# Rotary rotation inside PSUM, signs in the bank of sums, and three moves in the order of a post-norm transformer block

## The chip, the cores and the metric

The kernel runs on one core of a Trainium2 chip. The core has five engines with a queue of instructions each: TensorE (PE: matrix products, with its weight loads shown as PEld), VectorE (DVE), ScalarE (ACT), GpSimd (POOL) and SyncE (SP), which here only issues transfers. GpSimd issues transfers too, on a second queue. Matrix products are written to PSUM, eight banks of 128 partitions x 512 numbers of 32 bits; all other data on the core are in SBUF. The metric is the device time of one execution in microseconds (us), as the median over runs.

## The reference

One block: attention with 16 heads of width 32 that share one key and one value head, rotary positions on queries and keys, then a feed-forward part with ternary weights; a normalization without scale follows each. There are four batches (B = 4) of 512 positions (T = 512) and 512 channels (D = 512); the hidden width is 1408.

```python
q = (x @ Wq + bq).reshape(B, T, H, HD).transpose(0, 2, 1, 3)
k = (x @ Wk + bk)[:, None]
v = (x @ Wv + bv)[:, None]
q = _rotary(q, HD)
k = _rotary(k, HD)
scores = einsum('bhqd,bhkd->bhqk', q, broadcast(k)) / sqrt(HD)
attn = softmax(scores, axis=-1)
ctx = einsum('bhqk,bhkd->bhqd', attn, broadcast(v))
x = _layernorm(x + (ctx @ Wo + bo))
...
def _quantize(w):
    gamma = jnp.mean(jnp.abs(w))
    return jnp.clip(jnp.round(w / (gamma + EPS)), -1.0, 1.0)
hidden = sigmoid(x @ _quantize(w1).T) * (x @ _quantize(w2).T)
x = _layernorm(x + hidden @ _quantize(w3).T)
```

`_rotary` turns each pair (x1, x2) of the two halves of a head into (x1 cos - x2 sin, x2 cos + x1 sin).

## The kernel before, in words

**Main loop.** Work is cut into 64 steps (`steps`, line 678), numbered n: batch b, group of four heads c (NC = 4), chunk of 128 keys t (NT = 4). `PER` = 16 steps make a batch. In a step TensorE computes the scores of four heads with 128 keys (`scores`, line 375, tile `ps`), ScalarE takes the exponential (`es`), and TensorE weighs the values of the step before (`weigh`, tile `acc`). For the first batch TensorE also adds up the exponentials in every step (`count`, tile `den`); for the others GpSimd keeps running totals (`total`), and TensorE adds over them once in four steps (`normalize`, line 432).

**Maxima.** The softmax needs each row's maximum ahead of its scores. `find_maxima` (line 705) works LEAD = 7 steps ahead: TensorE computes the products (`pmax`), VectorE reduces them (`mx`). Called with two chunks, the products go to a tile of the pool `ps_sc`, whose two buffers of two banks serve the scores too; called with one, they go to the one bank tagged `den`, which also holds the sums. Line 763 chooses: two pairs per step while n < PER + 4, then single, pair, single.

**Projections.** `project_in` (line 237) makes keys, values and queries of a batch; its tiles `pk`, `pq` are in `ps_mm`, two buffers of one bank, which serve all other products too. `turn` (line 225) is the rotation. It gets the projection `src` in PSUM and a copy `r` (for the keys `kv`) that ScalarE makes in SBUF with the bias added. VectorE makes `a` = (src + bias) cos; after a yield it makes `w` = the copy with the halves of each head swapped (a shuffle), multiplies `w` by the signed sine, and adds `a` and `w`. The keys are stored four times, so a second addition writes the last 32 partitions.

**Fill.** `project_in`, `project_out` (line 517) and `feed_forward` (line 551) are generators; `Fill.draw` takes pieces of them between the fixed parts of a step, with about as much TensorE work as the step's `pace`. Each engine runs its instructions in the order of the program. `late` holds generators that `due` advances by one yield per slot, two slots a step: `spread` of the maxima, `normalize`, `layernorm`, `store_q`, `load_x`.

**Sums.** `normalize` copies the sums (`sums`), sends them through memory into a compact layout (`flat`, `few`), takes the reciprocal on VectorE, sends it back spread over the partitions (`rden`), and GpSimd multiplies `ctxT` by it. There is one yield between any two of these.

**Weights.** `quantized` (line 157) turns the three weight matrices, 11 tiles each, to ternary in 66 jobs: a first pass over each matrix sums absolute values on ScalarE (`junk`), a second takes the sign on ScalarE (`sgn`, bf16 in SBUF), and VectorE combines it (`raw`); the result is stored to memory (`kept`, the `w<-raw` transfers). GpSimd issues loads, four jobs ahead, and stores, from two pools of four and five buffers. Before the main loop, `quantize(3)` runs in each of seven rounds; inside, two or three jobs a step (lines 767, 769).

**Start.** SyncE issues the biases, `wkv_sb`, four `xT`, `wq_sb[0]`, `cos_sb`, `sin_sb`, and then the rest. GpSimd's first loads of `raw` stand right behind its memsets.

**End.** `feed_forward` splits the 11 hidden blocks into parts of 4, 4 and 3 (`parts`). For each block TensorE makes `gu` twice (gate and up), VectorE multiplies them (`hw`), and ScalarE and VectorE split the product into two halves `h`. After a part, TensorE multiplies it with the third matrix for the four tiles of 128 rows (`po`), and VectorE adds that to `x`. After the last part VectorE takes the statistics; in the last batch each tile is normalized and stored at once (`layernorm` with `root`).

Of the kernel before, what the change touches and what calls it, by code (L numbers as in the profile page):

```python
# [9 lines left out]
F32 = mybir.dt.float32  # L10
F32R = mybir.dt.float32r
BF16 = mybir.dt.bfloat16
# [7 lines left out]
P = 128  # L20
HD = 32
# [6 lines left out]
def postln_block(  # L28
# [75 lines left out]
    bq_sb = const.tile([P, NC], F32, name="bq_sb")  # L104
    bkv_sb = const.tile([P, 1], F32, name="bkv_sb")
    bo_sb = const.tile([P, D], F32, name="bo_sb")

    class Batch:
# [48 lines left out]
    def quantized():  # L157

        order = ((0, False), (1, False), (0, True), (2, False), (1, True), (2, True))
        jobs = [(m, last, f) for m, last in order for f in range(NF)]

        means = {}
        for n, (m, last) in enumerate(order):
            if not last:
                for k, step in ((2, 0), (6, 1), (10, 2)):
                    means[(n + 1) * NF + k] = (m, step)
        raws, part, row, pg, hi, waiting = {}, {}, {}, {}, {}, []

        def load(k):
            if k < len(jobs):
                m, _, f = jobs[k]

                tag, bufs = ("wd", 5) if k % 2 else ("wg", 4)
                raws[k] = wp.tile([P, W], F32, tag=tag, name="raw", bufs=bufs)
                pool.dma_start(out=raws[k], in_=wf[m, f])

        def mean(m, step):
            if step == 0:  # L180
                row[m] = small.tile([P, 1], F32, tag="row", name="row")
                dve.tensor_reduce(row[m], part[m], AX.X, ALU.add)
            elif step == 1:
                pg[m] = ps_mm.tile([P, 1], F32, tag="mm", name="pg")
                mm(pg[m], ones, row[m], True, True)
                gamma = small.tile([P, 1], F32, tag="gamma", name="gamma")
                act.activation(gamma, pg[m], AF.Identity, scale=1.0 / (NF * W * P), bias=eps_q)
                row[m] = gamma
            else:
                hi[m] = small.tile([P, 1], F32, tag="hi", name="hi")  # L190
                act.mul(hi[m], row[m], 0.5)

        AHEAD = 4
        for k in range(AHEAD):
            load(k)
        for k, (m, last, f) in enumerate(jobs):
            load(k + AHEAD)
            if k in means:
                mean(*means[k])
            raw = raws.pop(k)  # L200
            if not last:
                if f == 0:
                    part[m] = small.tile([P, NF], F32, tag="part", name="part", bufs=3)
                junk = work.tile([P, W], BF16, tag="th", name="junk")
                act.activation(junk, raw, AF.Abs, accum_out=part[m][:, f : f + 1])
            else:
                sgn = work.tile([P, W], BF16, tag="th", name="sgn")
                act.activation(sgn, raw, AF.Sign, bias=hi[m])
                dve.scalar_tensor_tensor(raw, raw, hi[m], sgn, ALU.is_gt, ALU.min)
                waiting.append((kept[m][f], raw))  # L210
            if len(waiting) > 2 or k + 1 == len(jobs):
                for w, q in waiting[: 1 if k + 1 < len(jobs) else 3]:
                    pool.dma_start(out=w.bitcast(F32), in_=q)
                del waiting[:1]
            yield
# [6 lines left out]
        act.copy(head, whole)  # L222
        pool.tensor_tensor(tail, whole, head.bitcast(F32), ALU.subtract)

    def turn(outs, src, bias, r, n):

        w = work.tile([P, T], F32, tag="rot_b", name="w")
        a = work.tile([P, T], F32, tag="rot_c", name="a", bufs=1)
        dve.scalar_tensor_tensor(a[0:n], src[0:n], bias[0:n], cos_sb[0:n], ALU.add, ALU.mult)
        yield  # L230
        dve.stream_shuffle(w[0:n], r[0:n], swap)
        dve.tensor_tensor(w[0:n], w[0:n], sin_sb[0:n], ALU.mult)
        for out, rows in outs:
            dve.tensor_tensor(out, a[rows], w[rows], ALU.add)
        yield

    def project_in(b):

        s = batches[b]
        n = P - HD  # L240
        while now < NC * NT * (b - 2):
            yield 0

        pk = ps_mm.tile([P, T], F32, tag="mm", name="pk")
        for c in range(NC):
            mm(pk, wkv_sb[:, c, :], s.xT[c], c == 0, c == NC - 1)
            if c == 1:
                yield -1.8
        kv = work.tile([P, T], F32, tag="rot_a", name="kv")
        act.activation(kv, pk, AF.Identity, bias=bkv_sb)  # L250
        s.kT = work.tile([P, T], F32, tag="kT", name="kT", bufs=3)
        rotation = turn(
            [(s.kT[0:n], slice(0, n)), (s.kT[n:P], slice(0, HD))], pk, bkv_sb, kv, n
        )
        next(rotation)
        yield 1.8
        next(rotation)
        if b > 0:
            late.append((slot + 2, split_k(b)))
        for c in range(NC):  # L260

            while b + 1 == B and c + 2 >= NC and not batches[0].projected:
                yield 0
            pq = ps_mm.tile([P, T], F32, tag="mm", name="pq")
            for d in range(NC):
                mm(pq, wq_sb[c][:, d, :], s.xT[d], d == 0, d == NC - 1)
                if d == 1:
                    yield -1.8
            r = work.tile([P, T], F32, tag="rot_a", name="r")
            act.activation(r, pq, AF.Identity, bias=bq_sb[:, c : c + 1])  # L270
# [7 lines left out]
            rotation = turn([(q, slice(0, P))], pq, bq_sb[:, c : c + 1], r, P)  # L278
            next(rotation)
            if c == 0:  # L280
                pv = ps_mm.tile([P, NT, HD], F32, tag="mm", name="pv")
                for t in range(NT):
                    transpose(pv[:, t, :], kv[n:P, ts(t, P)], ident[n:P, n:P])
                s.v = work.tile([P, NT, HD], F32, tag="v", name="v", bufs=3)
                act.copy(s.v, pv)
            yield 1.8
            next(rotation)
            if b > 0:
                late.append((slot + 2, store_q(b, c, q)))
            s.done = c + 1  # L290
        load_xT(NC if b == 0 else 2)

# [139 lines left out]
    def normalize(b, c):  # L432
# [12 lines left out]
        few = small.tile([P, NG * T // P], F32, tag="few", name="few")  # L445
        move(few, flat[0].rearrange("i (r j) -> (i r) j", r=HD))
        yield
        dve.reciprocal(few, few)
        move(flat[1].rearrange("i (r j) -> (i r) j", r=HD), few)
        yield  # L450
        rden = work.tile([P, T], F32, tag="rden", name="rden", bufs=1)
        for i in range(NG):
            move(rden[ts(i, HD), :], flat[1][i].partition_broadcast(HD))
        yield
        pool.tensor_tensor(s.ctxT[c], s.ctxT[c], rden, ALU.mult)
        yield

# [36 lines left out]
    def load_x(b):  # L494
        batches[b].x = []
        for t in range(NT):
            xt = xp.tile([P, D], F32, tag="x", name="xt")
            move(xt, x[b, ts(t, P), :])
            batches[b].x.append(xt)
        yield  # L500
        for xt in batches[b].x:
            pool.tensor_tensor(xt, xt, bo_sb, ALU.add)
        yield


    def split(head, tail, whole):
# [44 lines left out]
    def feed_forward(b):  # L551
# [1 line left out]
        s = batches[b]  # L553
        mv = small.tile([P, NT, 2], F32, tag="mv2", name="mv2")
        after = [(m, f) for f in range(NF) for m in range(2)][3:]
        parts = [range(f, min(f + 4, NF)) for f in range(0, NF, 4)]
        w3 = [[] for _ in parts]
        th = {}

# [21 lines left out]
        for k, fs in enumerate(parts):  # L581
# [15 lines left out]
            for t in range(NT):  # L597
# [27 lines left out]
    def store(b, t):  # L625
        move(out[b, ts(t, P), :], batches[b].x[t])
        yield
# [47 lines left out]
    def quantize(n):  # L675
        for _ in range(n):
            next(weights, None)
# [68 lines left out]
    for n, (b, c, t) in enumerate(steps):  # L746
# [94 lines left out]
```

## Time and profile before

| what | us |
|---|---|
| median of 3 runs (708.69 to 710.76) | 708.7 |
| profiled execution, its own time | 711.07 |
| span of the profiled execution, first to last instruction | 709.2 |
| TensorE busy in the span | 670.7 |
| VectorE busy | 409.4 |
| GpSimd busy | 326.8 |
| ScalarE busy | 297.2 |

The span is cut into 40 slices on the page; each digit is the busy share in tenths, PEclk the clock that TensorE was granted, in tenths of full speed, DMA the share of the transfer engines:

```profile
PE   7989999979879989999999999999998999999994
DVE  0897766868975564646554765455534333463334
POOL 3224433545977566639374474667573812202000
PEclk9999999989979989999999999999999999999998
DMA  8663877689734147427214247351130464235531
```

A slice is 17.7 us. TensorE's row is at 9 almost throughout and lower in the first slices, in slices 9, 11, 12 and 15, and in the last. Step 0 of the main loop starts at 50.5 us, step 16 (second batch) at 165.0, step 27 at 259.7, step 63 at 556.7; then the last batch's feed-forward part runs alone.

Groups of instructions that the change touches (busy us, mean ns of one, idle time before them and what ended it):

```profile
L74 DVE SCALAR_TENSOR_TENSOR raw<-raw,hi,sgn 128x512 f32<-128x512 f32 x33 | 26.3, 823 | 0.1
L74 ACT ACTIVATE sgn<-raw,hi 128x512 bf16<-128x512 f32 x33 | 22.8, 719 | 12.9 <-DVE raw L74 10.3 <-DMA raw<-in_wf 2.0 <-DVE mx L74 0.6
L74 DVE TENSOR_TENSOR w<-w,sin_sb 128x512 f32<-128x512 f32 x16 | 21.1, 1317 | 0.6
L74 DVE SCALAR_TENSOR_TENSOR a<-pq,bq_sb,cos_sb 128x512 f32<-128x512 f32 x16 | 11.9, 745 | 6.0 <-ACT r L74 5.9
L74 DVE TENSOR_TENSOR q<-a,w 128x512 f32<-128x512 f32 x12 | 11.9, 988 | 1.0
L74 DVE STREAM_SHUFFLE w<-r 128x512 f32<-128x512 f32 x16 | 11.7, 730 | 0.0
L74 ACT ACTIVATE r<-pq,bq_sb 128x512 f32<-128x512 f32 x16 | 10.9, 684 | 23.0 <-PE pq L79 19.1 <-issue 3.8
```

### The profile page before, as it was taken

How to read it: one execution, taken by the hardware profiler on the slowest of the kernel's cores; microseconds unless marked ns; L12 is line 12 of the kernel's file. 1: busy time of each engine (PE TensorE's matmuls, PEld its weight loads, DVE VectorE, ACT ScalarE, POOL GpSimd, SP SyncE). 2: the span in 40 equal slices, each digit the busy share in tenths (PEclk: the TensorE clock that was granted, in tenths of full speed). 3: DMA queues.
4: the chain of work that ended last, by engine and by line, in shares of the span. 5: the costliest groups of instructions: out<-in, count | busy, mean ns of one | idle time of the engine just before them, and what ended most of it. 6: DMA issues, size and time to landing. Idle time of an engine off the chain costs nothing.

```text
span 709.2 us, 9580 instructions
## 1 busy us (share of the span) xinstructions
PE 670.7 (95%) x3318; PEld 362.7 (51%) x3318; DVE 409.4 (58%) x577; ACT 297.2 (42%) x464; POOL 326.8 (46%) x412
## 2 busy tenths in 40 slices
PE   7989999979879989999999999999998999999994
PEld 5333333333324435556446565554454676768882
DVE  0897766868975564646554765455534333463334
ACT  1456657645423454424325445243434421224213
POOL 3224433545977566639374474667573812202000
PEclk9999999989979989999999999999999999999998
DMA  8663877689734147427214247351130464235531
GB/s 286 212 230 127 252 218 228 220 249 315 230 107 115 54 126 233 137 66 234 72 52 123 75 152 225 105 170 58 46 103 21 138 218 135 74 104 182 189 104 60
DMA packets 59663, 107.20 MB, mean 151 GB/s; under 512 B 13664, under 2 KB 14176, under 8 KB 59616
## 3 DMA queue, kind: packets, MB, share of 16 engines
q1 hardware_dynamic: 51696, 80.64, 36.5%
q0 software_dynamic: 7920, 25.96, 11.1%
q8 instruction: 26, 0.43, 0.2%
q14 instruction: 21, 0.17, 0.1%
HBM read 83.76 MB, written 22.81 MB: 150 GB/s over the span
## 4 chain that ended last, share of the span: by engine, by line
PE 77%; DVE 12%; DMA 2%; issue 2%; ACT 1%; SPq 1%; POOL 1%; DVEq 0%; ACTq 0%; POOLq 0%
PE gu L79 23%; PE po L79 19%; PE ps L79 11%; PE pmax L79 8%; PE acc L79 8%; PE pq L79 4%; PE den L79 3%; DVE mx L74 3%; DVE w L74 3%; DVE xt L74 1%; SPq L82 1%; DVE raw L74 1%; DMA few<-flat 1%; DMA rden<-flat 1%; PE pt L85 1%
## 5 line engine op out<-in xcount | busy, mean ns | idle before, releaser
L74 DVE TENSOR_REDUCE mx<-pmax 128x1 f32<-128x512 f32 (+1 forms) x165 | 159.1, 976 | 101.6 <-PE pmax L79 101.6
L74 ACT ACTIVATE es<-ps 128x1024 f32<-128x1024 f32 x128 | 124.1, 1021 | 132.6 <-PE ps L79 124.6
L79 PE MATMUL gu<-y,wg 128*128 128x512 f32 x704 | 173.1, 395 | 0.9 <-DVE xt L74 0.6
L79 PEld LDWEIGHTS gu<-y,wg 128*128 128x128 f32 x704 | 130.9, 188 | 39.8 <-issue 5.3
L74 POOL TENSOR_TENSOR total<-total,es 128x512 f32<-128x512 f32 x96 | 124.9, 1333 | 38.3 <-ACT es L74 38.1
L79 PE MATMUL po<-wd,h 128*128 128x512 f32 x352 | 90.9, 403 | 7.1 <-DVE xt L74 2.9
L74 POOL TENSOR_TENSOR total<-es 128x512 f32<-128x512 f32 x48 | 61.4, 1311 | 76.7 <-ACT es L74 76.7
L79 PE MATMUL pmax<-kr,qr 128*128 128x512 f32 x192 | 80.6, 478 | 3.2 <-DVE mx L74 2.4
L79 PEld LDWEIGHTS po<-wd,h 128*128 128x128 f32 x352 | 65.5, 190 | 30.3 <-DVE xt L74 5.3
L79 PE MATMUL acc<-es,v 128*32 128x512 f32 x512 | 70.8, 626 | 0.0
L79 PEld LDWEIGHTS pmax<-kr,qr 128*128 128x128 f32 x192 | 35.3, 192 | 60.0 <-issue 28.5
L74 DVE SCALAR_TENSOR_TENSOR hw<-th,gu 128x512 f32<-128x512 f32 x44 | 30.2, 687 | 57.5 <-PE gu L79 55.8
L74 DVE SCALAR_TENSOR_TENSOR xt<-po,xt 128x512 f32<-128x512 f32 x48 | 33.2, 691 | 51.8 <-PE po L79 51.7
L74 POOL DMA_DIRECT2D raw<-in_wf x66 | 35.8, 545 | 57.9 <-ACT junk L74 29.5
L74 ACT CAST h<-hw 128x512 fp32r<-128x512 f32 x44 | 27.3, 620 | 83.8 <-DVE hw L74 83.8
L79 PE MATMUL ps<-qT,kT 32*128 32x512 f32 x384 | 58.1, 660 | 4.2 <-DVE mx L74 4.2
L79 PE MATMUL po<-wo_sb,ctxT 128*128 128x512 f32 x128 | 61.4, 608 | 0.3 <-DVE hw L74 0.3
L79 PE MATMUL ps<-negm,ones_r 2*128 2x512 f32 x256 | 60.6, 810 | 0.0
L74 DVE TENSOR_TENSOR h<-hw,h 128x512 fp32r<-128x512 f32 x44 | 42.5, 965 | 26.4 <-ACT h L74 26.1
L79 PE MATMUL pq<-xT,wq_sb 128*128 128x512 f32 x112 | 53.6, 604 | 3.5 <-DVE m L74 1.5
L74 ACT ACTIVATE th<-gu 128x512 f32<-128x512 f32 x44 | 26.3, 597 | 46.2 <-PE gu L79 46.2
L79 PEld LDWEIGHTS po<-wo_sb,ctxT 128*128 128x128 f32 x128 | 24.3, 194 | 23.2 <-issue 20.8
(86 smaller groups left out, 646.9 us busy)
## 6 DMA issues: line engine op xcount, KB each, us to landing
wg<-w SPq DMA_DIRECT2D x88, 256.0 KB
raw<-in_wf POOLq DMA_DIRECT2D x66, 256.0 KB, 4.7
qr<-qp SPq DMA_DIRECT2D x96, 128.0 KB
wd<-w SPq DMA_DIRECT2D x44, 256.0 KB
w<-raw POOLq DMA_DIRECT2D x33, 256.0 KB, 4.8
qp<-q SPq DMA_DIRECT2D x48, 128.0 KB
rden<-flat SPq DMA_DIRECT2D x64, 64.0 KB
xt<-in_x SPq DMA_DIRECT2D x16, 256.0 KB
```

The source lines that it names most:

```text
L74: return lambda *args, **kw: pin(getattr(self.engine, name)(*args, **kw))
L79: pin(nc.tensor.matmul(out, lhsT=lhsT, rhs=rhs, start=start, stop=stop))
L82: pin(nc.sync.dma_start(out=out, in_=in_))
L85: pin(nc.tensor.transpose(out, in_, identity))
```

## The change

1. **Rotation.** For the first batch (`apart`) the rotation stays as it was, except that its copy `r` is made inside `turn`, and that the second addition for the keys, on 32 partitions, goes to GpSimd; in GpSimd's queue it stands ahead of the first loads of `raw`. From the second batch on there is no copy: VectorE makes `a`, swaps the halves inside the PSUM bank, multiplies there by the sine with the swapped bias `turned` added, and adds. All four are issued at once, ahead of the yield. `kv` holds the 32 rows of the values alone. The host appends the swapped biases to `bq` and `bkv`.
2. **Signs.** From step 17 on (`now > PER`) `sgn` is a float tile in the bank `den`.
3. **Pace of the weights.** Two jobs a step in the first batch, afterwards one, and two in every third step, instead of two and three in turn. The last job is thus in step 25 instead of 17.
4. **Maxima.** The two pairs per step last until the last batch's queries are made (through step 25) instead of through step 19, which leaves the bank `den` to the signs and sums.
5. **Sums.** For all but the last group of heads in a batch one more slot passes ahead of the reciprocal, and one ahead of the multiplication by `rden`.
6. **Bookkeeping.** `store_q` is put on `late`, and `done` counted, when the rotation is issued; `load_x` adds the bias to one tile per slot instead of four in one.
7. **End.** In the last batch the parts have 3, 4 and 4 blocks. A tile's normalization is issued after the next tile's statistics, and the last two after the last.

```diff
@@ quantized
-                sgn = work.tile([P, W], BF16, tag="th", name="sgn")
+                if now > PER:
+                    sgn = ps_acc.tile([P, W], F32, tag="den", name="sgn")
+                else:
+                    sgn = work.tile([P, W], BF16, tag="th", name="sgn")
@@ turn
-    def turn(outs, src, bias, r, n):
-        w = work.tile([P, T], F32, tag="rot_b", name="w")
-        a = work.tile([P, T], F32, tag="rot_c", name="a", bufs=1)
-        dve.scalar_tensor_tensor(a[0:n], src[0:n], bias[0:n], cos_sb[0:n], ALU.add, ALU.mult)
-        yield
-        dve.stream_shuffle(w[0:n], r[0:n], swap)
-        dve.tensor_tensor(w[0:n], w[0:n], sin_sb[0:n], ALU.mult)
+    def turn(outs, ps, bias, turned, n, apart):
+        a = work.tile([P, T], F32, tag="rot_c", name="a")
+        if apart:
+            r = work.tile([P, T], F32, tag="rot_a", name="r", bufs=1)
+            act.activation(r[0:n], ps[0:n], AF.Identity, bias=bias[0:n])
+        dve.scalar_tensor_tensor(a[0:n], ps[0:n], bias[0:n], cos_sb[0:n], ALU.add, ALU.mult)
+        if apart:
+            yield
+            w = work.tile([P, T], F32, tag="rot_b", name="w", bufs=1)
+            dve.stream_shuffle(w[0:n], r[0:n], swap)
+            dve.tensor_tensor(w[0:n], w[0:n], sin_sb[0:n], ALU.mult)
+        else:
+            w = ps
+            dve.stream_shuffle(ps[0:n], ps[0:n], swap)
+            dve.scalar_tensor_tensor(ps[0:n], ps[0:n], turned[0:n], sin_sb[0:n], ALU.add, ALU.mult)
         for out, rows in outs:
-            dve.tensor_tensor(out, a[rows], w[rows], ALU.add)
+            engine = pool if apart and out.shape[0] == HD else dve
+            engine.tensor_tensor(out, a[rows], w[rows], ALU.add)
         yield
@@ project_in
-        kv = work.tile([P, T], F32, tag="rot_a", name="kv")
-        act.activation(kv, pk, AF.Identity, bias=bkv_sb)
+        kv = work.tile([P, T], F32, tag="kv", name="kv", bufs=1)
+        act.activation(kv[n:P], pk[n:P], AF.Identity, bias=bkv_sb[n:P, 0:1])
...
-            yield 1.8
-            next(rotation)
             if b > 0:
                 late.append((slot + 2, store_q(b, c, q)))
+                s.done = c + 1
+            yield 1.8
+            next(rotation, None)
             s.done = c + 1
@@ normalize
         yield
+        if c + 1 < NC:
+            yield
         dve.reciprocal(few, few)
...
         yield
+        if c + 1 < NC:
+            yield
         pool.tensor_tensor(s.ctxT[c], s.ctxT[c], rden, ALU.mult)
@@ load_x
         for xt in batches[b].x:
             pool.tensor_tensor(xt, xt, bo_sb, ALU.add)
-        yield
+            yield
@@ feed_forward
-        parts = [range(f, min(f + 4, NF)) for f in range(0, NF, 4)]
+        short = NF % 4 if b + 1 == B else 0
+        ends = sorted({0, NF, *range(short, NF, 4)})
+        parts = [range(*pair) for pair in zip(ends, ends[1:])]
...
                     if b + 1 == B:
-                        for _ in layernorm(s.x[t : t + 1], mv[:, t : t + 1, :], True):
-                            pass
-                        late.append((slot + 1, store(b, t)))
+                        for done in range(max(t - 1, 0), t if t + 1 < NT else NT):
+                            for _ in layernorm(s.x[done : done + 1], mv[:, done : done + 1, :], True):
+                                pass
+                            late.append((slot + 1, store(b, done)))
@@ main loop
-        if n < PER + 4:
+        if batches[-1].done < NC:
             find_maxima(n + LEAD, 0, 1)
             due()
             find_maxima(n + LEAD, 2, 3)
-            quantize(2)
+            quantize(1)
             fill.draw(pace)
-            quantize(n % 2)
+            quantize(1 if b == 0 or n % 3 == 0 else 0)
```

More of the change, by code (lines that the diff above doesn't have):

```diff
@@ L103, in postln_block @@
     wo_sb = const.tile([P, NC, D], F32, name="wo_sb")
-    bq_sb = const.tile([P, NC], F32, name="bq_sb")
-    bkv_sb = const.tile([P, 1], F32, name="bkv_sb")
+    bq_sb = const.tile([P, 2 * NC], F32, name="bq_sb")
+    bkv_sb = const.tile([P, 2], F32, name="bkv_sb")
     bo_sb = const.tile([P, D], F32, name="bo_sb")
@@ L248, in project_in @@
                 yield -1.8
-        kv = work.tile([P, T], F32, tag="rot_a", name="kv")
-        act.activation(kv, pk, AF.Identity, bias=bkv_sb)
+        kv = work.tile([P, T], F32, tag="kv", name="kv", bufs=1)
+        act.activation(kv[n:P], pk[n:P], AF.Identity, bias=bkv_sb[n:P, 0:1])
         s.kT = work.tile([P, T], F32, tag="kT", name="kT", bufs=3)
         rotation = turn(
-            [(s.kT[0:n], slice(0, n)), (s.kT[n:P], slice(0, HD))], pk, bkv_sb, kv, n
+            [(s.kT[0:n], slice(0, n)), (s.kT[n:P], slice(0, HD))],
+            pk, bkv_sb[:, 0:1], bkv_sb[:, 1:2], n, b == 0,
         )
@@ L268, in project_in @@
                     yield -1.8
-            r = work.tile([P, T], F32, tag="rot_a", name="r")
-            act.activation(r, pq, AF.Identity, bias=bq_sb[:, c : c + 1])
             if b == 0:
@@ L277, in project_in @@
                 q = work.tile([P, T], F32, tag="q", name="q")
-            rotation = turn([(q, slice(0, P))], pq, bq_sb[:, c : c + 1], r, P)
+            rotation = turn(
+                [(q, slice(0, P))], pq, bq_sb[:, c : c + 1], bq_sb[:, NC + c : NC + c + 1], P, b == 0
+            )
             next(rotation)
@@ L285, in project_in @@
                 act.copy(s.v, pv)
-            yield 1.8
-            next(rotation)
             if b > 0:
                 late.append((slot + 2, store_q(b, c, q)))
+                s.done = c + 1
+            yield 1.8
+            next(rotation, None)
             s.done = c + 1
@@ L811, with swapped @@
     bk, bv = np.asarray(L0_attn_bk), np.asarray(L0_attn_bv)
+    bkv = np.concatenate([bk, bk, bk, bv])[:, None]
+    bq = np.asarray(L0_attn_bq).reshape(-1, P).T
+    def swapped(a):
+        return a.reshape(P // HD, 2, HALF, -1)[:, ::-1].reshape(a.shape)
     ins = {
@@ L815 @@
         "wq": np.asarray(L0_attn_Wq).reshape(NC, P, NC, P).transpose(1, 2, 0, 3),
-        "bq": np.asarray(L0_attn_bq).reshape(-1, P).T,
+        "bq": np.concatenate([bq, swapped(bq)], axis=1),
         "wkv": np.concatenate([wk, wk, wk, wv], axis=1).reshape(NC, P, P).transpose(1, 0, 2),
-        "bkv": np.concatenate([bk, bk, bk, bv])[:, None],
+        "bkv": np.concatenate([bkv, swapped(bkv)], axis=1),
         "wo": L0_attn_Wo,
```

## The prediction

> **What bounds the kernel now.** I read the page's busy times first: TensorE 95% busy, VectorE 58%. So TensorE sets the span, and what can be won is its idle time and the time in which its clock is down. The windows view (columns: stretch, length, then busy time and count of PE, PEld, DVE, ACT, POOL, then granted clock, DMA share, GB/s) says where these lie.
>
> ```profile
> PE 670.7 (95%) x3318; PEld 362.7 (51%) x3318; DVE 409.4 (58%) x577; ACT 297.2 (42%) x464; POOL 326.8 (46%) x412
> ```
> ```profile
> 0.00:20.00 20.00, 15.46 (x68) 10.15 (x68) 3.45 (x6) 3.02 (x5) 5.45 (x18) 1.00 0.87 298
> ...
> 145.00:165.00 20.00, 16.42 (x74) 5.78 (x72) 10.70 (x16) 8.34 (x11) 7.49 (x13) 0.83 0.83 255
> 165.00:191.00 26.00, 23.41 (x110) 9.28 (x109) 25.59 (x36) 14.70 (x22) 20.18 (x23) 1.00 0.78 257
> 191.00:214.00 23.00, 18.42 (x69) 6.63 (x68) 17.70 (x11) 6.78 (x9) 17.64 (x14) 0.78 0.44 139
> ...
> 250.00:276.00 26.00, 22.46 (x120) 11.29 (x116) 15.44 (x21) 11.31 (x16) 16.59 (x13) 0.87 0.62 190
> ...
> 693.00:709.20 16.20, 6.25 (x24) 3.97 (x22) 8.68 (x22) 5.37 (x11) 0.00 (x0) 0.87 0.17 65
> ```
>
> Four places lose time: the start (4.5 us idle), 145 to 214 (10.8 us idle, clock down to 0.83 and 0.78), 250 to 276, and the end. The timeline shows each cause (start, duration, engine, line, instruction; in brackets the idle time before it and what ended it).
>
> ```profile
> 1.60 4.47 POOL L74 DMA_DIRECT2D raw<-in_wf  x8
> ...
> 13.47 1.12 PE L79 MATMUL pk<-xT,wkv_sb 128*128 128x512 f32 x2 [0.78 <-DMA xT<-in_xT]
> ...
> 15.42 3.67 PE L79 MATMUL pq<-xT,wq_sb 128*128 128x512 f32 x8 [0.82 <-DMA wq_sb<-in_wq]
> ```
> ```profile
> 153.43 0.25 DVE L74 RECIPROCAL few<-few 128x16 f32<-128x16 f32 x1 [4.14 <-DMA few<-flat]
> ...
> 154.82 2.35 PE L79 MATMUL ps<-room,kT 32*128 32x512 f32 x6 [3.58 <-DVE mx L74]
> ...
> 187.91 4.94 POOL L74 TENSOR_TENSOR total<-total,es 128x512 f32<-128x512 f32 x4
> ...
> 190.78 7.53 DVE L74 TENSOR_TENSOR w<-w,sin_sb 128x512 f32<-128x512 f32 x1
> 192.82 4.93 POOL L74 TENSOR_TENSOR xt<-xt,bo_sb 128x512 f32<-128x512 f32 x4
> ...
> 201.17 2.35 PE L79 MATMUL ps<-qT,kT 32*128 32x512 f32 x6 [4.24 <-DVE mx L74]
> ```
>
> Early on, eight weight loads of GpSimd share the transfers with what the first projections need. At 153 VectorE stands 4.14 us for the sums' round trip, the maxima behind it are late, and TensorE waits 3.58. At 190 one multiply takes 7.53 us, spanning GpSimd's two rows of four additions, and TensorE waits 4.24. After both waits TensorE runs at half rate (six `ps` 2.35 us; elsewhere eight take 1.14). The tiles view explains the multiply: VectorE's instructions with one input in PSUM never stretch (`xt<-po,xt` 683 to 692 ns over 48), those with two in SBUF do (`w<-w,sin_sb` 686 to 7530).
>
> **The change, part by part.** The starts of the score groups give the length of each step n of the main loop; TensorE keeps nearly the same fill work in each step, so steps compare. Steps 4 to 13 average 6.72 us; 14 and 15 take 10.05 and 10.16, 19 and 20 take 10.14 and 12.92.
>
> *Start.* GpSimd adds the last quarter of the first keys and only then issues its loads. That addition needs `w`, so the 2 MB leave the stretch that counts. Shared, the last two input chunks came 1.91 us apart (pk's rows at 11.56 and 13.47); alone, `wq_sb` and `cos_sb` came 0.96 apart (15.42 and 16.38). Counting back five transfers of 1.93 from 15.42 puts the first at 5.8, so transfers run from about 3.9. At 0.96 each, the six up to `wq_sb` land at 9.7, cosine and sine by 11.6. pk then runs unbroken from 8.79 for two rows of 1.88, pq from 12.55 instead of 15.42: **-2.9**. VectorE keeps pace: pq ends at 16.2, r at 16.95, four operations (0.75, 0.72, 0.69, 0.69) bring the first queries to 19.9, before 22.86. The moved addition, 1.37 by the 64-row `kr` row, runs 16.2 to 17.6 beside pq; the second shuffle waits for it but is due only at 17.7. The loads issue from 17.6; the first `junk`, due near 21.7, has its tile at about 21.5 (two for issue and latency, 1.9 shared). Behind `junk` on ScalarE stands the third r, due at 27.8; ScalarE idles 4.35 before it now, which covers a late tile. Bounds 0 (loads late) to -4.
>
> *Reciprocal one slot later.* A slot is half a step, 3.3 us; of 4.14 some 0.9 stays, too little to pass on to TensorE (1.9 of fill lie between). Also two weight tiles a step are quantized instead of 2.5, so transfers thin out. Steps 14 and 15 fall to the mean: 3.3 + 3.4 = 6.8, less 0.9: **-5.9**, bounds -2 to -6.8.
>
> *Rotation in PSUM, and the bias additions of x one per slot.* Gone are w's and q's additions with two SBUF inputs and ScalarE's r (0.68 each). VectorE does a, shuffle, multiply, addition: 0.745 + 0.73 + 0.745 + 0.69 = 2.91, against 3.78 by the means now (0.745, 0.73, 1.317, 0.988). No row has VectorE write to PSUM; below stands 0.67 (`y<-pt,y`), above 1.32 (stretched w), I take the shuffle's and a's own, as those read PSUM or write the same count. Step 19's other work is 5.9 (scores 1.3, weighing 1.0, maxima 1.1, fill 1.9, waits 0.65) and step 20's is 8.0 (step 21's 7.0 plus 1.0 for den): 4.2 + 4.9 = **-9.1**, bounds -3 to -10.5 (steps 17 and 18 too). The longer hold of the projection's bank is hidden by two slots: the next tile needs it 3.6 us of fill later. In steps 25 to 28 the stretched w and q (1.23, 1.57) stand in the chain before `y`; TensorE stalls 2.38 and 1.07 and runs at half rate to 267. I take 1.4 for the rows and 0.6 of the slow clock: **-2**, bounds 0 to -5.
>
> [...]
>
> *Paired maxima in steps 20 to 25.* While signs use the sums' bank, maxima go through the score buffers in pairs and wait for ScalarE's second exponential. In step 19, weighing ends at 193.4 and the pairs start at 193.56 and 194.48, one pair needing 0.46: 0.65 lost. Where den or pm lies between, 0.2 or 0.4. Two steps each: **+2.5**, bounds 0 to +4.
>
> *Signs in PSUM.* ScalarE writes twelve tiles to one bank, each waiting until `raw` of the one before has been read. Priced nothing: ScalarE is 42% busy, and `raw` goes ahead of the rotation on VectorE. Uncovered, each costs 0.75 plus a pair of maxima, 1.2: at most +4 for two.
>
> *Short part first at the end.* After the last up product, its two halves must be made before the last output rows, 2.9 us (692.8 to 695.70), then VectorE runs four tiles 2.38 apart. With four blocks in the last part, eight more matmuls of 0.226 lie in that shadow, so the product ends 1.8 us earlier. VectorE's chain stays at 10.4: per tile 1.65 plus 0.35 of the tile before, but the third normalization now goes ahead of the fourth on ScalarE. **-1.8**, bounds 0 to -2.5.
>
> Sum: -2.9 - 5.9 - 9.1 - 2 + 2.5 - 1.8 = -19.2. The profiled execution took 711.07 us, its span 709.2; 690.0 in span. The median shown, 708.7, is 2.4 below that execution, so the same difference leads to about 689.5; I say 690.
>
> **Rivals.** *VectorE stays late.* The four operations now stand in one block ahead of the next step's maxima, where before only a did. Without den, TensorE offers the pair after 1.3 + 1.0 + 0.46 = 2.76 us, while block and `raw` need 3.66; after 2.4 of maxima TensorE may be 0.6 late. Over 15 rotations that is 9: 699. For it: VectorE at 25.59 of 26 us in 165 to 191. Against: from 50 to 145 it holds 74% without holding up TensorE.
>
> *The start gains nothing*, since the late loads stall ScalarE or the transfers are not what limits: 693. Against it stand the two spacings.
>
> *GpSimd takes over as the bound.* From 165 to 250 it is busy 60.7 us; eight loads and eight stores at 0.545, until now done by step 15, come on top: 69.4 of the 78 that these steps would last. Loads wait in order for an earlier store to land (5.2 and 5.7 us the longest now), with the totals queued behind, and behind these the exponentials' buffers. From two such waits on GpSimd decides; six make 69.4 + 32.4 = 101.8, hence 690 + 24 = 714. Against: the store a load waits for is issued two tiles earlier, and at 1.33 tiles a step of 7.8 us that is 11.7 us, while the longest landing is 7.9.
>
> **How the numbers follow.** Forecast 67%, VectorE late 20%, no gain at the start 6%, GpSimd 7%. 682 has all terms near their better bounds; 704 holds the second case with margin. No change means within 0.3%, 2.1 us: about what a measurement of this kernel can tell. Faster 0.87; same 0.04, slower 0.09 (GpSimd's 7% and the far end of VectorE late).
>
> **What would show it.** pq starting near 12.6; steps 14 and 15 below 7.5 and no idle before `ps` of over 1 us at 145 to 205; in-place shuffle and multiply at 0.7 to 0.75; granted clock near 1 there; steps 22 and 23 at 7.5 instead of 6.85; last up product ending 1.8 us earlier before the end. The forecast is wrong if the in-place instructions take over 1 us, if `raw` loads on GpSimd wait beside the totals, or if `es` waits behind `sgn`.

## The result, and the profile after

The changed kernel takes 700.14 us (median of 4 runs, 699.91 to 701.57) against 708.7 us, a ratio of 0.9864 with a 95% interval of 0.9832 to 0.9896. That is 1.4% faster; the forecast was 690. The profiled execution took 699.91 us, its span 698.1 us, 11.1 less than before. Where they went, by the starts of the steps (us; "e9" is the best of the experiments' orders, told of below):

| stretch | before | after | difference | forecast | e9 less before |
|---|---|---|---|---|---|
| up to step 0 | 50.46 | 49.69 | -0.8 | -2.9 | -2.8 |
| steps 0 and 1 | 13.98 | 18.76 | +4.8 | 0 | 0.0 |
| steps 2 to 13 | 80.33 | 79.64 | -0.7 | 0 | +0.1 |
| steps 14 and 15 | 20.21 | 13.03 | -7.2 | -5.9 | -7.2 |
| steps 16 to 18 | 26.05 | 24.87 | -1.2 | 0 | -1.0 |
| steps 19 and 20 | 23.06 | 21.36 | -1.7 | -9.1 | -7.2 |
| steps 21 to 25 | 35.69 | 38.45 | +2.8 | +2.5 | +2.7 |
| steps 26 to 28 | 26.37 | 21.95 | -4.4 | -2 | -4.0 |
| steps 29 to 62 | 280.53 | 280.45 | -0.1 | 0 | -0.1 |
| step 63 to the end | 152.52 | 149.90 | -2.6 | -1.8 | -2.6 |

Two stretches account for the miss: the first steps and steps 19 and 20. The windows view after, cut at steps 14 to 15 and 19 to 20 (stretch, length, then busy time and count of PE, PEld, DVE, ACT, POOL, then granted clock, DMA share, GB/s):

```profile
148.09:161.12 13.03, 13.03 (x75) 5.76 (x74) 10.25 (x15) 7.22 (x10) 6.14 (x12) 1.00 0.78 248
...
185.99:207.35 21.36, 17.07 (x70) 5.35 (x69) 10.15 (x13) 7.16 (x10) 16.19 (x18) 1.00 0.47 152
```

Steps 14 and 15 have no idle TensorE left. Steps 19 and 20 still have 4.3 us of it, nearly as large a gap as before (4.6), though the clock is up from 0.78 to 1.00. The rotation inside PSUM costs what the forecast took; VectorE's groups from 60 to 300 us (busy us, mean ns of one, idle time before them):

```profile
L74 DVE SCALAR_TENSOR_TENSOR pq<-pq,bq_sb,sin_sb 128x512 f32<-128x512 f32 x12 | 9.1, 759 | 0.4
L74 DVE SCALAR_TENSOR_TENSOR a<-pq,bq_sb,cos_sb 128x512 f32<-128x512 f32 x12 | 8.9, 744 | 3.8 <-PE pq L79 3.8
L74 DVE STREAM_SHUFFLE pq<-pq 128x512 f32<-128x512 f32 x12 | 8.3, 694 | 0.0
L74 DVE TENSOR_TENSOR q<-a,pq 128x512 f32<-128x512 f32 x12 | 8.3, 688 | 0.9
```

They sum to 2.89 us per rotation against the forecast's 2.91. So the miss is not there. It is in what stands behind other work in a queue. First, step 0. The timeline after (start, duration, engine, line, instruction; in brackets the idle time before it and what ended it):

```profile
44.82 0.74 DVE L74 SCALAR_TENSOR_TENSOR a<-pk,bkv_sb,cos_sb 96x512 f32<-96x512 f32 x1
...
47.00 1.38 DVE L74 TENSOR_TENSOR kT<-a,pk 96x512 f32<-96x512 f32 x2
48.40 2.36 DVE L74 TENSOR_REDUCE mx<-pmax 128x2 f32<-128x1024 f32 x2
...
49.69 2.03 PE L79 MATMUL ps<-room,kT 32*128 32x512 f32 x6 [1.69 <-DVE mx L74]
...
56.62 3.78 PE L79 MATMUL pq<-spare,wq_sb 128*128 128x512 f32 x4
```

And the same place before:

```profile
47.35 0.74 DVE L74 SCALAR_TENSOR_TENSOR a<-pk,bkv_sb,cos_sb 96x512 f32<-96x512 f32 x1
48.00 2.34 DVE L74 TENSOR_REDUCE mx<-pmax 128x2 f32<-128x1024 f32 x2
...
50.27 0.71 DVE L74 STREAM_SHUFFLE w<-kv 96x512 f32<-96x512 f32 x1
```

Before, only `a` of the second batch's keys stood ahead of the last maxima, and the shuffle came behind. Now the whole rotation of the keys, five instructions from 44.82 to 48.40, stands ahead. The scores, whose buffers the maxima still hold, wait 1.69 us; then TensorE runs at half rate (four `pq` products 3.78 us, 1.98 before; the granted clock in step 0 is 0.57, 1.00 before). Up to 46 us the start had been 2.5 us ahead of before; step 0 takes 4.3 longer and spends it.

Second, step 20, in the timeline after:

```profile
194.83 1.28 POOL L74 TENSOR_TENSOR ctxT<-ctxT,rden 128x512 f32<-128x512 f32 x1 [5.08 <-DMA rden<-flat]
196.07 1.28 POOL L74 TENSOR_TENSOR xt<-xt,bo_sb 128x512 f32<-128x512 f32 x1
197.31 4.92 POOL L74 TENSOR_TENSOR total<-total,es 128x512 f32<-128x512 f32 x4
...
194.96 0.51 PE L79 MATMUL ps<-negm,ones_r 2*128 2x512 f32 x4 [1.99 <-DMA negm<-rows]
...
198.62 1.05 PE L79 MATMUL den<-total,ones 128*32 128x512 f32 x2 [1.30 <-POOL total L74]
```

And the same multiplication before:

```profile
199.51 1.60 POOL L74 TENSOR_TENSOR ctxT<-ctxT,rden 128x512 f32<-128x512 f32 x1
```

After, GpSimd stands 5.08 us for `rden`, with step 19's last totals queued behind; TensorE needs these totals for `den` and goes at GpSimd's pace, two of the eight products after each addition. Before, the multiplication found its data there. TensorE waits here for `negm` as well.

### The profile page after: what moved, and what is told of

It is laid out like the page before. It is cut to its first block, busy times and chain, and to the rows that moved or that the text cites. A ratio compares the mean times of both kernels' runs of the same rounds, so it can differ in the third digit from the quotient of the medians.

```text
span 698.1 us, 9545 instructions
## 1 busy us (share of the span) xinstructions
PE 668.9 (96%) x3318; PEld 362.2 (52%) x3318; DVE 394.0 (56%) x570; ACT 290.1 (42%) x453; POOL 323.6 (46%) x413
## 4 chain that ended last, share of the span: by engine, by line
PE 84%; DVE 8%; DMA 2%; ACT 2%; issue 2%; POOL 1%; SPq 1%; ACTq 0%; DVEq 0%; POOLq 0%
PE gu L79 24%; PE po L79 19%; PE ps L79 12%; PE pmax L79 8%; PE acc L79 8%; PE pq L79 6%; PE den L79 4%; DVE mx L74 3%; PE pk L79 1%; DVE xt L74 1%; PE warm L79 1%; ACT es L74 1%; DMA rden<-flat 1%; POOL total L74 1%; DMA xt<-in_x 1%
## 5 line engine op out<-in xcount | busy, mean ns | idle before, releaser
L79 PE MATMUL pmax<-kr,qr 128*128 128x512 f32 x192 | 75.0, 453 | 2.2 <-ACT es L74 1.6
L79 PE MATMUL acc<-es,v 128*32 128x512 f32 x512 | 68.2, 605 | 0.0
L79 PEld LDWEIGHTS pmax<-kr,qr 128*128 128x128 f32 x192 | 33.7, 188 | 56.1 <-issue 21.4
L79 PE MATMUL ps<-negm,ones_r 2*128 2x512 f32 x256 | 59.0, 787 | 2.0 <-DMA negm<-rows 2.0
L79 PE MATMUL po<-wo_sb,ctxT 128*128 128x512 f32 x128 | 59.1, 594 | 0.3 <-DVE hw L74 0.3
L79 PE MATMUL ps<-qT,kT 32*128 32x512 f32 x384 | 55.7, 640 | 0.0
```

The lines of the kernel that those rows point to most:

```text
L79: pin(nc.tensor.matmul(out, lhsT=lhsT, rhs=rhs, start=start, stop=stop))
```

## The experiments

Twelve kernels ran, each the changed kernel with the edit that is shown. Nine of them have a single time and are read by their steps. They ran on three chips, on which the kernel before took 710.9 us (median of seven runs; e1_keys to e4_loads), 714.9 (one run; e5_sbuf to e8_ln) and 709.7 (seven; e9_slots2 to e12_filled); a difference of 1 or 2 us between single times shows nothing by itself.

**e1_keys: only the keys' `a` ahead of the maxima, as before.**

```diff
             w = ps
+            if n < P:
+                yield
             dve.stream_shuffle(ps[0:n], ps[0:n], swap)
```

> Only the keys' rotation from the second batch on is split again: a is issued, the shuffle and the rest one piece of fill later, behind the maxima. Theory (the block of four operations ahead of the maxima makes TensorE wait 1.69 us at 49.7, and after that wait it runs at half rate): the wait goes, step 0 falls from 10.66 to about 6.4 us, and the main loop's step 2 starts 5 to 6 us earlier; time about 694.5. Rival (the half rate comes from the sparse products of the first 50 us, now 2.5 us earlier, not from this wait): the wait goes, but step 0 keeps more than 9 us; time 698.

700.07 us. The wait for the maxima is gone (`ps` at 48.06, 1.6 us earlier), but step 0 still takes 9.13 us: TensorE's clock halves one wait later (granted 0.69 in step 0). The timeline of e1_keys:

```profile
50.54 2.99 PE L79 MATMUL pmax<-kT,room 32*128 32x512 f32 x8 [1.11 <-ACT es L74]
53.46 3.78 PE L79 MATMUL pq<-spare,wq_sb 128*128 128x512 f32 x4
```

Before has the same wait (1.10 us) without the loss. The 3.1 us that were won by the start of step 2 are given back in several places: step 20 takes 16.61 us, 1.1 more than after, step 27 1.0 more, and steps 2 to 13 0.7.

**e2_ctx: the multiplication by `rden` one slot later for every group of heads, so behind step 19's totals.**

```diff
-        if c + 1 < NC:
-            yield
+        yield
         pool.tensor_tensor(s.ctxT[c], s.ctxT[c], rden, ALU.mult)
```

> The last group's multiplication by rden comes one slot later too, so it stands behind step 19's totals in GpSimd's queue instead of ahead of them. Theory (GpSimd's 5.08 us wait for rden holds up the totals, and these the sums on TensorE): step 20 falls from 15.5 to 8.5 to 10 us, den starts within 2 us of the first pair of maxima; time about 694. Rival (the transfers' lateness holds step 20 by itself, as the 1.99 us wait for negm shows): step 20 stays above 13 us, with TensorE waiting for ctxT instead; time 698 to 700.

695.37 us. The timeline of e2_ctx:

```profile
191.02 4.95 POOL L74 TENSOR_TENSOR total<-total,es 128x512 f32<-128x512 f32 x4
195.94 1.27 POOL L74 TENSOR_TENSOR ctxT<-ctxT,rden 128x512 f32<-128x512 f32 x1
...
196.67 1.07 PE L79 MATMUL den<-total,ones 128*32 128x512 f32 x8
```

GpSimd's totals and `ctxT` do not wait, `den` is one row of eight at 1.07, and step 20 falls from 15.52 to 9.98 us; the time falls by 4.8. TensorE still waits 1.47 us for `negm`, and keeps its full rate behind that wait. Step 0 is as after (10.93).

**e3_both: the two together.**

> Both edits. If the two losses are independent, their gains add: about 5.5 plus 6, hence 688 to 690 against 700.1. If they share a cause (GpSimd or the transfers late as a whole), no better than the better one alone: 694.

690.08 us (4 runs, 688.26 to 693.49), ratio 0.9712 (0.9657 to 0.9767). Step 0 takes 6.38 us, as before the change, behind the same 1.11 us wait at which e1_keys lost its clock (granted 1.00 here). Step 20 takes 11.77; the timeline of e3_both shows what is left:

```profile
180.59 1.98 SPq L82 DMA_DIRECT2D rden<-flat  x4
182.61 1.08 SPq L82 DMA_DIRECT2D negm<-rows  x2
...
187.69 0.51 PE L79 MATMUL ps<-negm,ones_r 2*128 2x512 f32 x4 [1.72 <-DMA negm<-rows]
```

`negm`, due at once, is issued behind four transfers of `rden`; TensorE waits 1.72 us and then runs `den` at half rate (1.93 against 1.07 in e2_ctx, behind a wait of 1.47).

**e9_slots2: e3_both, with the reciprocal one slot later for every group too, which puts `negm` ahead of `rden`.**

```diff
-        if c + 1 < NC:
-            yield
+        yield
         dve.reciprocal(few, few)
```

> The kernel of e3_both, and the reciprocal of the next batch's sums one slot later as well (a yield ahead of both multiplications in every chunk), so that in SyncE's queue the transfer of negm no longer follows the transfer of rden at step 20. Theory (TensorE's 1.72 us wait for negm at step 20, and the half rate behind it, come from that order): the wait goes, step 20 takes 8.0 to 8.5 us instead of 11.8, the rest stays as in e3_both; time 685 to 688. Rival (the row rden only lands later, and ctxT and then po wait for it instead): the waiting moves to step 21 or to GpSimd ahead of the next totals; time 690 or more.

689.15 us (688.78 to 690.43), ratio 0.9707 (0.9675 to 0.9739). The theory holds for the wait and fails for the time. In the timeline of e9_slots2 `negm` goes first and step 20 has no wait for it; `ctxT` is now the late one, by 0.50 us, and the eight `den` take 2.12 us, since the last of GpSimd's totals ends at 190.13 while they run (from 189.11):

```profile
177.38 1.07 SPq L82 DMA_DIRECT2D negm<-rows  x2
179.47 1.71 SPq L82 DMA_DIRECT2D rden<-flat  x4
...
194.97 1.13 PE L79 MATMUL po<-wo_sb,ctxT 128*128 128x512 f32 x2 [0.50 <-POOL ctxT L74]
```

Step 20 takes 10.06 us. The 1.7 us are given back elsewhere: the start is 0.4 longer than in e3_both's profile, step 17 0.7 and step 61 1.0, so the spans agree (687.1 and 687.2). Against the runs of before that each shared a chip with, the two kernels cannot be told apart.

**e12_filled: e9_slots2, with work for TensorE in the short wait of step 0.**

```diff
         es = scores(b, c, t)
+        if n == 0:
+            filler = ps_acc.tile([P, P], F32, tag="den", name="filler")
+            for _ in range(18):
+                mm(filler, ones_r, ones_r, True, True)
```

> The kernel of e9_slots2 with 18 products of ones by ones (128x128 each, their sum is not used) on TensorE behind the scores of step 0, in the 1.1 us in which it waits for the exponentials. Theory (the half rate of step 0 follows from that short wait, and whether it comes differs from one execution to the next): with the wait filled the rate never halves there, step 0 takes 6.4 to 7 us in the profile and the times stand within about 1.5 us of each other. Rival (the filling costs as much as it saves, or the rate is decided elsewhere): step 0 takes 9 us or more all the same, or the times spread as those of e3_both (688.3 to 693.5).

688.70 us (687.99 to 688.84), ratio 0.9695 (0.9658 to 0.9732), the best value measured; the intervals of e9_slots2 and e12_filled overlap. The timeline of e12_filled:

```profile
48.52 2.22 PE L79 MATMUL filler<-ones_r 128*128 128x128 f32 x18
50.67 1.14 PE L79 MATMUL pmax<-kT,room 32*128 32x512 f32 x8
51.75 1.98 PE L79 MATMUL pq<-spare,wq_sb 128*128 128x512 f32 x4
```

The eight `pmax` take 1.14 us instead of 2.04, but the filler costs as much: step 0 takes 6.46. The times stand within 0.85 us of each other, as the theory has it. Since e9_slots2 kept its clock in step 0 in its profile too, and its times span only 1.65 us, this is consistent with the theory and does not show it.

**e4_loads: the second addition of the first keys, which writes their last 32 partitions, on VectorE again, so the early loads are not held back.**

```diff
-            engine = pool if apart and out.shape[0] == HD else dve
+            engine = dve
```

> The 32 rows of the first keys are added on VectorE again, so GpSimd's first loads are issued at 1.6 us. Theory of the prediction (these loads share the transfers): pq starts near 15.4 instead of 12.9, the main loop's step 0 would start 2.5 us later if nothing else changed. Since the wait and the half rate of step 0 come from the block of four operations, they stay: time about 702 to 703. Rival (the earlier start is what brings about the half rate of step 0): step 0 falls to 6.4 and the time is 698 or less.

701.35 us. `pq` starts at 15.54 (15.42 before, 12.91 after) and step 0 at 52.38 instead of 49.69: 2.7 us, the size that the forecast gave to the start. Steps 0 and 1 give 1.1 of it back.

**e5_sbuf: the rotation of the later batches in SBUF again, from a copy by ScalarE, issued as one block like in the change.**

```diff
-        if apart:
+        if True:
             r = work.tile([P, T], F32, tag="rot_a", name="r", bufs=1)
...
-            w = ps
-            dve.stream_shuffle(ps[0:n], ps[0:n], swap)
-            dve.scalar_tensor_tensor(ps[0:n], ps[0:n], turned[0:n], sin_sb[0:n], ALU.add, ALU.mult)
+            w = work.tile([P, T], F32, tag="rot_b", name="w", bufs=1)
+            dve.stream_shuffle(w[0:n], r[0:n], swap)
+            dve.tensor_tensor(w[0:n], w[0:n], sin_sb[0:n], ALU.mult)
```

> The rotation from the second batch on keeps its four VectorE operations in one block but makes them in SBUF, from a copy r by ScalarE, as the first batch does; all else as in the changed kernel. Theory (VectorE's instructions with two inputs in SBUF are held up by GpSimd's additions, and PSUM avoids it): w and q stretch again, some beyond 1.3 us, and steps 16 to 19 and 25 to 27 together take 3 to 7 us more (50.1 now); time 703 to 707. Rival (what freed these steps is the slower pace of the weights and x's additions being spread): the operations stretch little, the steps stay within 1 us; time 700.

702.14 us. No 7.53 us row comes back: the longest multiplication by the sine takes 0.91, the longest addition of queries 1.60. Steps 16 to 19 take 31.10 us (30.71 after, 36.19 before). Step 26 is longer by 1.1. Step 20 is longer by 1.4, but it takes 15.9 to 16.6 us in e1_keys, e4_loads, e7_parts and e8_ln too, which keep the rotation in PSUM. So PSUM itself is worth at most about 2 us in the changed kernel, not the 11 that were put down to it.

**e11_unspread: e5_sbuf, with all bias additions of x in one slot again.**

```diff
             pool.tensor_tensor(xt, xt, bo_sb, ALU.add)
-            yield
+        yield
```

> The changed kernel with batch two's rotation in SBUF, as in e5_sbuf, and GpSimd's two bias additions of a load of x in one slot again. Theory (VectorE's operations on SBUF stretch while GpSimd runs additions without a gap): the stretched rows come back, a multiplication by the sine or the last addition longer than 3 us, and steps 18 to 20 longer than those of e5_sbuf by 2 us or more; time 704 to 708. Rival (the additions' slot does nothing by itself): no row above 1.8 us, steps 18 to 20 as in e5_sbuf, time 701 to 703.

700.85 us. The theory falls. One rotation now stands beside GpSimd's additions of x, which follow one another without a gap as before the change. In the timeline of e11_unspread its multiplication by the sine takes 0.88 us:

```profile
184.75 5.88 POOL L74 TENSOR_TENSOR xt<-xt,bo_sb 128x512 f32<-128x512 f32 x4
...
185.69 0.88 DVE L74 TENSOR_TENSOR w<-w,sin_sb 128x512 f32<-128x512 f32 x1
```

Here it is GpSimd that is stretched, 5.88 us for four additions instead of 4.93. The longest addition of queries is again 1.60, one of the keys' reaches 1.74, and steps 18 to 20 take 29.70 us against 31.52 in e5_sbuf. The spreading of these additions is not what ended the 7.53 us row. It has another effect: with the four additions ahead of it again, GpSimd's multiplication by `rden` (194.14) finds its data, where it waited 6.01 us in e5_sbuf. The totals behind it start late all the same (195.50), and step 20 takes 15.12.

**e6_slots: without the slots ahead of the reciprocal and of the multiplication.**

```diff
-        if c + 1 < NC:
-            yield
         dve.reciprocal(few, few)
...
-        if c + 1 < NC:
-            yield
         pool.tensor_tensor(s.ctxT[c], s.ctxT[c], rden, ALU.mult)
```

> The extra slots ahead of the reciprocal and of the multiplication by rden are taken out for all groups. Theory of the prediction (the slot ahead of the reciprocal took away its wait at 153): VectorE waits 3 us or more for few near step 14 again, TensorE idles and then runs at half rate, steps 14 and 15 take 9 to 10 us each instead of 6.7 and 6.3; time 705 to 708. Rival (two weight tiles a step instead of 2.5 thin the transfers enough): few lands in time, steps 14 and 15 stay below 7; time 700.

705.77 us. Steps 14 and 15 stay short, 6.73 and 6.19. What gets longer is step 17, 12.59 us instead of 8.27, and step 27, 8.88 instead of 5.92; step 20 is shorter by 1.2. Why step 27 is longer was not followed. The timeline of step 17 in e6_slots, GpSimd, then SyncE, then TensorE:

```profile
162.09 1.28 POOL L74 TENSOR_TENSOR ctxT<-ctxT,rden 128x512 f32<-128x512 f32 x1 [4.77 <-DMA rden<-flat]
163.33 1.28 POOL L74 TENSOR_TENSOR q<-q,q 128x512 fp32r<-128x512 f32 x1
...
164.64 1.73 SPq L82 DMA_DIRECT2D qp<-q  x4
166.47 3.76 SPq L82 DMA_DIRECT2D qr<-qp  x2
170.33 1.54 SPq L82 DMA_DIRECT2D xT<-in_xT  x2
...
175.90 2.91 PE L79 MATMUL pk<-xT,wkv_sb 128*128 128x512 f32 x4 [3.13 <-DMA xT<-in_xT]
```

The slots are worth 5.6 us by this one time, and not where they were expected: GpSimd waits in order for `rden`, the query halves behind it are late, SyncE waits in order for the halves, and the input of the next batch is issued late. The margin is small: after, `xT` is issued at 168.92, and TensorE waits 0.42 us for it.

**e10_pace: the old pace of the weights.**

```diff
-            quantize(1)
+            quantize(2)
             fill.draw(pace)
-            quantize(1 if b == 0 or n % 3 == 0 else 0)
+            quantize(n % 2)
```

> The changed kernel with the old pace of the weights' quantizing (two halves and then n % 2 a step). Theory (steps 14 and 15 became short since GpSimd had less to quantize there, not since the reciprocal stands one slot later): steps 14 and 15 go back to 9 to 10 us each, time 704 to 707. Rival (the reciprocal's slot alone cured them): steps 14 and 15 stay at about 6.5 us, time 698 to 701.

699.58 us; steps 14 and 15 take 6.52 and 6.43. So the slower pace alone is not what shortened these steps either. The slots and the pace were not taken out together, so that either of them suffices is not excluded. Step 17 has a 3.12 us wait for `xT` (12.41 us) with the slots in place, `xT` being issued at 169.99; step 20 is 3.0 shorter than after, step 61 1.4 and step 27 0.7, so the time is that of the changed kernel.

**e7_parts and e8_ln: the end.** The one takes the last batch's parts back to 4, 4 and 3 blocks, the other normalizes each tile right behind its own statistics.

```diff
-        short = NF % 4 if b + 1 == B else 0
+        short = 0
```

```diff
-                        for done in range(max(t - 1, 0), t if t + 1 < NT else NT):
+                        for done in (t,):
```

> The last batch has parts of 4, 4 and 3 blocks again; the new order of the normalizations stays. From the start of step 63 to the end: 149.9 us in the changed kernel, 152.5 before. Theory of the prediction (the short part first brings 1.8): 151.7, time 702. Rival (the order of the normalizations brings nearly all of it, since VectorE's chain, not TensorE, sets the end): 150.3 or less, time 700.5.

> Each tile of the last part is normalized right after its own statistics again; parts of 3, 4 and 4 stay. Theory (the order brings what the short part does not, 2.6 less 1.8): from the start of step 63 to the end 150.7 us, the four additions to x spaced 2.4 us instead of 1.9; time 701. Rival (the order brings nearly all): 152 or more, time 702.5.

From step 63 to the end e7_parts takes 151.43 us and e8_ln 150.57, against 149.90: the short part is worth 1.5 us, the order of the normalizations 0.7 (VectorE's additions of the last tiles stand 2.41 apart in e8_ln, 1.87 after). Their times, 701.08 and 702.19, are single runs and hold the start's scatter too.

## Why the prediction was right, and where it was wrong

*Right in sign and bounds, 10 us too low in size.* About 690 is what the change gives once two blocks are issued later (e3_both 690.1, e9_slots2 689.2): the gains were mostly there, and two waits that the forecast left out of its sum took 10 to 11 us of them. That the sum comes so close then is in part luck: steps 14 and 15 and steps 26 to 28 gained more than was forecast and steps 19 and 20 less, and for these terms the cause that was given is not borne out. It is luck, too, that the time lies next to the 699 of the rival "VectorE stays late": that came from 0.6 us in each of 15 rotations, and the time went in two places, of which one is such a block.

*Start, -2.9.* Size right: -2.5 until 46 us, and e4_loads loses 2.7. The first load was there at most 3.4 us after its issue (18.45, first `junk` 21.87), where the forecast allowed 3.9, two of them the author's estimate for issue and latency. ScalarE waited for a late load once, 2.01 us at 25.2, and its next `r` was not held up. The failed point is what came next: "The four operations now stand in one block ahead of the next step's maxima" was named as a rival for the 15 rotations of the later batches and left out of the sum. It held once, at step 0, where the keys' block is five instructions and the last maxima of the start are due at once. It took 1.7 us ahead of step 0 and 4.8 in steps 0 and 1 instead of 0.6, since the half rate comes on top of the wait.

*Reciprocal one slot later, -5.9.* The stretch fell by 7.2, and the reason that was given is not borne out: with the slot taken out it stays short (e6_slots), with the old pace too (e10_pace), though not tried with both. The 4.14 us for `few` can be followed in SyncE's timeline of before:

```profile
135.82 0.52 SPq L82 DMA_DIRECT2D flat<-sums  x1
136.44 0.40 SPq L82 DMA_DIRECT2D qw<-q  x1
140.81 1.84 SPq L82 DMA_DIRECT2D qp<-q  x4
142.69 1.51 SPq L82 DMA_DIRECT2D qT<-qw  x1
144.30 1.99 SPq L82 DMA_DIRECT2D qr<-qp  x2
146.33 1.12 SPq L82 DMA_DIRECT2D few<-flat  x1
```

Before, 10.5 us lie between `flat` and `few`, because a store of queries whose halves were not ready stands between them; in e6_slots 3.1 (139.21 and 142.26), after 2.3, in e10_pace 4.7. From the issue of `few` to the reciprocal another 7.1 us pass before. So most of the sums' round trip had passed when its second half was issued. The order of SyncE's queue comes from several parts of the change together (the rotation issued as one block, the query store put on the list earlier); which one is needed was not tried.

*Rotation in PSUM, -9.1 in steps 19 and 20, -2 behind 25.* Step 19 fell by 4.3 (4.2 expected), steps 26 to 28 by 4.4. Step 20 was to fall by 4.9 and rose by 2.6. The failed step is the 8.0 us for step 20's other work, "step 21's 7.0 plus 1.0 for den": it counted TensorE's and VectorE's work and took GpSimd's as unchanged. But spreading the additions of x takes three of them away from in front of the multiplication by `rden`, and the slot ahead of that multiplication, which the forecast left without a price, is absent for a batch's last group of heads. There GpSimd now reaches the multiplication before its data and stands 5.08 us; with the slot (e2_ctx) step 20 takes 9.98 us. The rival "GpSimd takes over as the bound" was close, with the wrong wait: not loads behind stores but `ctxT` behind `rden`, with the totals queued behind, as it said of the loads. And the cause that the forecast gave for the rest is not borne out: with the rotation in SBUF again step 19 takes 5.84 us (e5_sbuf) and 5.83 (e11_unspread), as after, and steps 26 to 28 22.38 and 24.00, against 21.95 after and 26.37 before. Nor is it enough that GpSimd adds without a gap beside VectorE, since the multiplication then took 0.88 us in e11_unspread and 1.74 one step later in the kernel before (at 203.59, beside 5.39 us of totals). What brought about the one row of 7.53 us, and which part of the change ended it, stays open. What PSUM is worth while GpSimd runs its totals beside, as in e9_slots2, was not tried.

*Paired maxima, +2.5.* Measured +2.8 in steps 21 to 25, each of 21 to 23 longer by 0.6 to 0.7. *Signs in PSUM, 0.* `sgn` takes 0.69 us in the bank, `raw` 0.74 as median, and ScalarE stood 3.4 us in all for `raw`, which cannot be told, in the steps from 21 on, from the pairs' 0.6. *Short part first, -1.8.* Measured 1.5 by e7_parts; the last up product ends 134.43 us behind step 63's start instead of 136.25, the 1.8 that were predicted. The normalizations' order, priced at nothing, brought 0.7 more.

*PSUM as a source.* Beside SBUF it cost at most some 15 ns in these rows: before, `a`, which reads PSUM, takes 745 ns as mean and `raw`, which reads SBUF, 744 as median; after, `a` stays at 744 ns, the multiplication in place takes 759, and a shuffle from PSUM to PSUM takes 694 ns, less than the 730 from SBUF to SBUF before.

## What to carry to other kernels

Where instructions are moved on an engine that issues in order, look up what each waiting instruction has queued behind it, on every queue it feeds: step 0, step 20, the sums' round trip and step 17 of e6_slots were all such queues, on engines half idle. A row that is several times its usual length can be gone without the change that was made against it, as the 7.53 us row was in e5_sbuf and e11_unspread; so take that change back alone before it is given the credit. Give the wait that is left over a slot at the place that is due last, and check the last element of a loop apart: here the exception for a batch's last group of heads cost 4.8 us.

## What the runs showed of the hardware

TensorE's half rate did not follow from the program alone. Behind a wait of 1.1 us in step 0 the same order of TensorE's instructions ran at full rate before, in e3_both and in e9_slots2 (`pq` 1.98), and at half rate in e1_keys (3.78); behind the block's wait for the maxima, 1.69 to 1.88 us in nine of the profiles, the rate fell each time (the four `pq` 3.78 us after and in e8_ln, 2.98 in e7_parts, 2.80 in e11_unspread). In step 20 it halved behind a wait of 1.72 us in e3_both (eight `den` 1.93) and not behind 1.47 in e2_ctx (1.07) and 1.99 after (granted clock 1.00). One short wait of 1.1 us in step 0 thus cost between nothing and 2.8 us. What brings the clock down behind one wait and not behind another was not tried.

GpSimd's addition of the first keys on 32 partitions took 1.70 us, more than its usual 1.28 on 128; it ran beside VectorE's addition of the other 96 (16.68 to 17.37 us), which has two SBUF operands as well. The forecast's 1.37 was too low.

VectorE's addition of two SBUF operands still stretched to 1.60 us beside GpSimd in e5_sbuf (the queries' addition took 0.69 as median before), and none with a PSUM operand did after (686 to 690 ns over 12). Why the one stretches, these rows do not show.
